# Pair-wise cross-attention mixture kernel: softmax weights turned by VectorE, first x loaded by rows, later x loaded earlier, GpSimd's setup reordered

## The chip, the core and the metric

The kernel runs on one NeuronCore of one Trainium2 chip. The metric is the device time of one execution, in microseconds, and the number to predict is the median of timed executions. Engine names below are those of the profile: PE is TensorE (PEld its weight loads), DVE is VectorE, ACT is ScalarE, POOL is GpSimd, and SP is SyncE, which here only issues DMAs.

## What is computed

x has shape (8, 512, 256): 8 batches of 512 tokens, with 64 context vectors for each batch and one conditioning vector, the anchor. All of it is 32-bit. In short:

```
nx       = layer_norm(x, gamma, beta)
weights  = softmax((nx @ Wq) (context @ Wk)^T / 16)          # 512 x 64 for each batch
evidence = weights @ (context @ Wv)
combined = [nx, evidence, anchor]                             # 768 wide
probs    = softmax(combined @ router_W + router_b)            # 3 experts
h_e      = silu(combined @ e_w1[e] + e_b1[e])                 # 768 -> 512, for each expert
routed   = sum_e probs_e * (h_e @ e_w2[e] + e_b2[e])          # 512 -> 256
g        = sigmoid(silu(combined @ gate_w1 + gate_b1) @ gate_w2 + gate_b2)
out      = x + g * (routed @ out_w + out_b)
```

## The kernel before

**Folding.** The key and query matrices are joined into one, so the scores are one product of nx with a 256 x 64 matrix for each batch. The value matrix is folded into the evidence rows of the first layers (`vw`), so the product with the evidence becomes a product of the softmax weights `wT` (64 context rows by 512 tokens) with `vw`. The second layers are folded with `out_w` (`w2o`). The router's softmax needs only logit differences against expert 0.

**Pairs.** The eight batches are handled as four pairs `j`. A pair is a 2 x 2 block matrix (two halves of the features by two batches), and each product of it is done with seven block products in place of eight. The extra sums and differences of weights are made once by POOL (`combine_weights`, `ws`), those of x by DVE or POOL (`combine_x`, tile `T`).

**Stages of a pair.** `gate_layer` makes the hidden layer of the gate. `expert_layer` runs three times, for the three experts, with the points "W", "A", "B", "C" and "D" at which other steps are hung. `outputs` does the second layers, with the points "begin", "gate", "P1" to "P7". The lists `within` and `between` at the end of the program say which step is run at which point: the next pair's statistics, normalization, scores, softmax and router logits lie between the products of the current pair. Every engine runs its instructions in the written order, and SP's DMAs are issued in the written order too.

**Names that matter below.**
- `load_x` (L139) loads one tile x by four DMAs of 32 partitions; partition quarter (i, h) holds half h of the tokens of batch i of the pair. With this layout the softmax weights, made with tokens on partitions in 32 x 32 blocks, have their router sums by token. The tag "x" has two buffers, so pair j+1's two tiles wait for the readers of pair j's.
- `statistics`, `deviation`, `normalize` (L528 to L550) are the layer norm; `store_x`, `regroup_x` and `transpose_blocks` bring x of later pairs into the transposed form `nxT` through DRAM; `transpose_x` (L562) does it by TensorE for the first pair.
- `router_part` (L586) makes the last logit difference of a tile from x and a row `gg`, by four DVE instructions. For the first pair it is hung at "gate".
- `scores` (L628), `softmax` (L659) and `turn_weights` (L666): the weights w are normalized with tokens on partitions; `turn_weights` transposes them in 32 x 32 blocks into `tw`, and DMAs carry the blocks to the partitions of `wT`. For the first pair four DMAs are issued by ACT, after two DVE transposes; for later pairs eight are issued by SP.
- `router_logits` (L682) needs the router's rows `vr`, which go from `vw` through DRAM (`store_router_rows`, `spread_router_rows`, both on POOL's queue), and `rbias`, which goes the same way (`router_anchor`, `spread_router_bias`).
- `misc` (L104) hands out PSUM banks in turn from a short list, so a new user of a bank waits for the readers of the one before.

Of the kernel before, what the change touches and what calls it, by code (L numbers as in the profile page):

```python
# [8 lines left out]
F32 = mybir.dt.float32  # L9
# [7 lines left out]
def kernel(  # L17
# [121 lines left out]
    def load_x(b):  # L139
        x_sb[b] = xpool.tile([P, NT, H], F32, tag="x", name=f"x_{b}")  # L140
        j, a = b // 2, b % 2
        for i, h in SIDES:
            nc.sync.dma_start(x_sb[b][side(i, h), :, :], tile_rows(x[2 * j + i], a, h))
# [15 lines left out]
    def by_k(flat, n):  # L159
# [16 lines left out]
        scr[:, NL : NL + 3 * KH * E].rearrange("p (k e) -> p k e", e=E),  # L176
        scr[:, NL + P : NL + P + KH * ED].rearrange("p (k e) -> p k e", e=ED),
        scr[:, NL + 2 * P : NL + 2 * P + B],
# [94 lines left out]
    nc.gpsimd.memset(rw2, 0.0)  # L273
    nc.gpsimd.tensor_copy(rw2[:, :, 1:], rwd[:, :KH, 1:])
    nc.gpsimd.tensor_tensor(rb_c[:, 0:1], rb_c[:, 0:1], rb_c[:, 1:], ALU.subtract)
# [98 lines left out]
    def router_anchor():  # L374
        ps = misc("ps_rb")
        for k in range(KH):
            nc.tensor.matmul(
                ps[:ED, :B], rwd[:, 2 * KH + k, :], condT[:, k, :B], start=(k == 0), stop=(k == KH - 1)
            )
        for k in range(KH):  # L380

            nc.tensor.matmul(
                ps[:ED, B : B + 1], rw2[:, k, :], beta_c[:, k : k + 1], start=(k == 0), stop=(k == KH - 1)
            )
        nc.vector.tensor_scalar(rcol, ps[:ED, B : B + 1], rb_c[:, 0:1], None, ALU.add)
        nc.vector.tensor_scalar(
            rrow.rearrange("e (i j) -> e j i", i=2), ps[:ED, :B].rearrange("e (j i) -> e j i", i=2),
            rcol, None, ALU.add,
        )
        nc.gpsimd.dma_start(rbd.rearrange("i j e -> e (i j)"), rrow)  # L390
# [171 lines left out]
    def transpose_x(b):  # L562
        j, a = b // 2, b % 2
        xn = S["xn", b]
        for k in range(KH):
            if a == 0:
                row = 2 * j + k
                S["nxT", row] = npool.tile([P, KH, T], F32, tag="nxT", name=f"nxT_{row}")
        for k in range(KH):
            pt = misc(f"pt_x_{b}_{k}")  # L570
            for t in range(NT):
                nc.tensor.transpose(pt[:, t * P : (t + 1) * P], xn[:, t, k * P : (k + 1) * P], ident)
            src = pt.rearrange("p (j i h r) -> p i h j r", i=2, h=2, r=TB)
            for i in range(2):
                dst = S["nxT", 2 * j + i][:, k, :]
                dst = dst.rearrange("p (h a j r) -> p a h j r", h=2, a=2, r=TB)[:, a]
                scale_x(dst, k, src[:, i], k % 2 == 0)

# [7 lines left out]
    def router_part(b):  # L586

        j, a = b // 2, b % 2
        lg = logits(j)
        junk = work.tile([P, H], F32, tag="tw", name=f"junk_{b}", bufs=1)  # L590
        for t in range(NT):
            nc.vector.scalar_tensor_tensor(  # L592
                junk, S["xn", b][:, t, :], 1.0, gg, ALU.mult, ALU.mult,
                accum_out=lg[:, 2, a * NT + t : a * NT + t + 1],
            )
# [32 lines left out]
    def scores(j):  # L628


        ps = misc(f"ps_s_{j}")
        for g in range(2):
            for k in range(KH):
                for i, h in SIDES:
                    nc.tensor.matmul(
                        ps[side(i, h), g * NH : (g + 1) * NH],
                        mr[:, k, 2 * j + i, g * TB : (g + 1) * TB],
                        S["nxT", 2 * j + i][:, k, h * NH : (h + 1) * NH],
                        start=(k == 0),
                        stop=(k == KH - 1),  # L640
                    )
        w = work.tile([P, 2, NJ, TB], F32, tag="w", name=f"w_{j}", bufs=1)
        S["w", j] = w
        nc.vector.transpose(w.rearrange("p g j c -> p (g j c)"), ps)
        nc.vector.tensor_copy(logits(j)[:, 1, :], w[:, 0, :, 0])
        nc.vector.memset(w[:, 0, :, 0], 0.0)
        mx = work.tile([P, NJ], F32, tag="mx", name=f"mx_{j}")
        nc.vector.tensor_reduce(mx, w.rearrange("p g j c -> p j g c"), AX.XY, ALU.max)
        nmx = work.tile([P, NJ], F32, tag="nmx", name=f"nmx_{j}")
        nc.vector.tensor_scalar_mul(nmx, mx, -SCALE)  # L650
        sm = work.tile([P, NJ], F32, tag="sm", name=f"sm_{j}")
        for t in range(NJ):
            nc.scalar.activation(
                w[:, :, t, :], w[:, :, t, :], AF.Exp, bias=nmx[:, t : t + 1], scale=SCALE,
                accum_out=sm[:, t : t + 1],
            )
        S["sm", j] = sm

    def softmax(j):  # L659
        w, sm = S["w", j], S.pop(("sm", j))  # L660
        rs = work.tile([P, NJ], F32, tag="rs", name=f"rs_{j}")
        nc.vector.reciprocal(rs, sm)
        rs = rs.unsqueeze(1).unsqueeze(3).to_broadcast([P, 2, NJ, TB])
        nc.vector.tensor_tensor(w, w, rs, ALU.mult)

    def turn_weights(j, queue, twice=False):  # L666

        tw = work.tile([P, 2, NH], F32, tag="tw", name=f"tw_{j}", bufs=1)
        nc.vector.transpose(
            tw.rearrange("p g t -> p (g t)"), S["w", j].rearrange("p g j c -> p (g j c)")  # L670
        )
        wT = work.tile([P, T], F32, tag="wT", name=f"wT_{j}", bufs=1)
        S["wT", j] = wT
        if twice:

            nc.vector.transpose(wT, S["w", j].rearrange("p g j c -> p (g j c)"))
        for i, h in SIDES:
            for g in range(2):
                if not twice or g != h:
                    queue.dma_start(wT[side(i, g), h * NH : (h + 1) * NH], tw[side(i, h), g, :])  # L680

    def router_logits(j):  # L682
        w, lg, vr = S["w", j], S["lg", j], S["vr", j]
        le = work.tile([P, ED, NJ], F32, tag="le", name=f"le_{j}")
        for e in range(ED):
            pv = work.tile([P, 2, NJ, TB], F32, tag="tw", name=f"pv_{j}_{e}", bufs=1)
            nc.vector.tensor_tensor(
# [173 lines left out]
    def gate_layer(j, steps):  # L861
# [12 lines left out]
        keep_part(n, 1, 1, Z[n])  # L874
        if j == 0:
            turn_weights(0, nc.scalar, twice=True)
        nx_product(j, n, 2, True)
# [300 lines left out]
    with tc.manual_schedule(engines=None):  # L1178
# [36 lines left out]
        store_router_rows(0)  # L1215
        spread_router_bias()
        combine_weights(E)
        spread_router_rows(0)
        transpose_x(1)
        combine_x(0, nc.vector, (0, 1))  # L1220
        scores(0)
        load_table(AF.Silu)
        combine_weights(0)
        softmax(0)
        value_weights(0, 0, nc.vector.tensor_copy)
        anchor_rows(E)
        anchor_rows(0)
        combine_x(0, nc.vector, (2, 3))
        combine_weights(1)
# [9 lines left out]
        for j in range(NP):  # L1239
# [7 lines left out]
            if j == 0:  # L1247
                put(within, "gate", router_part, 0)
                put(within, "gate", router_part, 1)
                put(within, "gate", value_weights, 0, 1)  # L1250
# [20 lines left out]
            if j:  # L1271
                put(within, "gate end", spread_probabilities, j)
            put(within, (0, "C" if j == 0 else "B"), value_weights, j, 2)
            put(within, (1, "C"), load_x_blocks, 2 * j)
            put(within, (2, "A"), gate_differences, j)
            put(within, (2, "C"), load_x_blocks, 2 * j + 1)
            if j + 1 < NP:
                b0, b1 = 2 * j + 2, 2 * j + 3
                put(within, "gate", load_x, b0)
                put(within, "gate", load_x, b1)  # L1280
                put(within, (0, "A" if j else "D"), statistics, b0, 0, NT)
                put(within, (0, "B") if j else (1, "A"), statistics, b1, 0, NT)
                for i in range(2):
                    put(within, (0, "D") if j else (1, "C"), deviation, j + 1, i)
                for b, n in ((b0, (1, "W") if j else (1, "D")), (b1, (1, "A") if j else (2, "W"))):
                    put(within, n, normalize, b)
                    put(within, n, store_x, b)
                put(within, (1, "C") if j else (2, "A"), regroup_x, b0)
                put(within, (1, "B") if j else (2, "A"), router_part, b0)
                put(within, (2, "W") if j else (2, "B"), router_part, b1)  # L1290
                put(between, "begin", transpose_blocks, b0)
# [9 lines left out]
                put(between, "P7", router_logits, j + 1)  # L1301
                put(between, "P7", turn_weights, j + 1, nc.sync)
                put(between, "P3", value_weights, j + 1, 1)
                put(between, "P3", router_exp, j + 1)
                put(between, "P4", router, j + 1)
# [38 lines left out]
```

## Time and profile before

| | |
|---|---|
| timed runs | 496.11, 498.0 and 501.9 us, median 498.0 |
| the profiled execution | 503.33 us, of which 501.5 us is the span from its first to its last instruction |
| granted TensorE clock, mean | 0.975 |
| PE, DVE, ACT, POOL busy | 94%, 72%, 43%, 19% of the span |
| setup and first gate layer | 0 to 54.5 us |
| pair 0 from expert 0 to its outputs' end | 54.5 to 171 us |
| pairs 1, 2, 3 | from 171, 285 and 394 us |

The profiled execution is slower than the slowest timed run by 1.4 us, so differences worked out from its rows are taken from 503.33, and the same difference is then taken from the median. In a row of the timeline the first number is the start and the second the duration of the group (both in us), then come engine, line, operation, tiles, and in brackets the idle time of the engine before it with what ended it. A 128x512 product is two PE records in this trace, which at full rate start 0.43 us apart.

### The profile page before, as it was taken

What the parts mean: (1) busy time and instruction counts of PE and PEld (TensorE: products, weight loads), DVE (VectorE), ACT (ScalarE), POOL (GpSimd) and SP (SyncE); (2) the same over time, 40 slices, a digit from 0 to 9 for tenths busy, and PEclk for the clock granted to TensorE, in tenths of its full rate; (3) what the DMA queues carried; (4) which work ended last, traced back from release to release, by engine and by line L of the source; (5) the groups of instructions that cost most, each with busy time, mean ns of one, the idle gap of its engine ahead of it and who ended that gap; (6) DMA issues with size and microseconds to landing.
All of it is one profiled execution on the core that took longest, in us unless ns stands there. A gap on an engine that the chain in (4) does not pass through costs nothing.

```text
span 501.5 us, 4762 instructions
## 1 busy us (share of the span) xinstructions
PE 473.0 (94%) x1439; PEld 213.6 (43%) x1439; DVE 361.6 (72%) x668; ACT 215.2 (43%) x385; POOL 96.9 (19%) x132
## 2 busy tenths in 40 slices
PE   8874999997999996999999998999999999999996
PEld 6531354632444442443444443443444444444454
DVE  2854474797879935789888954988979925787972
ACT  2440465543822253655822154745622364468000
POOL 5239012410107220000107230000108210000020
PEclk9988799998999998999999999999999999999999
DMA  9995723034201272181201182470201391000013
GB/s 216 286 171 112 136 35 127 1 90 78 43 5 21 40 193 64 48 141 22 43 5 22 36 195 64 100 111 0 42 7 21 60 211 25 0 0 1 0 21 64
DMA packets 120795, 35.81 MB, mean 71 GB/s; under 512 B 106605, under 2 KB 117793, under 8 KB 120257
## 3 DMA queue, kind: packets, MB, share of 16 engines
q1 hardware_dynamic: 116560, 27.81, 29.3%
q0 software_dynamic: 2128, 6.78, 4.3%
q10 hardware_dynamic: 2080, 0.92, 0.7%
q8 instruction: 11, 0.18, 0.2%
q14 instruction: 16, 0.12, 0.1%
HBM read 27.17 MB, written 7.39 MB: 69 GB/s over the span
## 4 chain that ended last, share of the span: by engine, by line
PE 59%; DVE 20%; DMA 12%; SPq 5%; issue 2%; ACT 1%; DVEq 0%
PE ps_u L774 30%; PE ps_z L774 11%; PE ps_y L774 9%; DMA x<-in_x_dram 5%; DMA ow_sb<-in_L_xcond_out_w_dram 4%; DVE h L1051 4%; PE ps_gu L774 3%; DVE h L858 3%; DVE junk L592 2%; PE ps_vw L749 2%; SPq L680 2%; SPq L1073 2%; PE ps_w2o L489 1%; PE ps_gz L774 1%; DMA w<-in_L_xcond_e_w_dram 1%
## 5 line engine op out<-in xcount | busy, mean ns | idle before, releaser
L858 DVE TENSOR_TENSOR h<-h,pb 128x512 f32<-128x512 f32 x96 | 62.0, 696 | 9.2 <-ACT h L807 9.2
L774 PE MATMUL ps_u<-h,w2o 128*128 128x512 f32 x144 | 64.1, 594 | 0.0
L807 ACT ACTIVATE h<-h,abias 128x512 f32<-128x512 f32 x72 | 49.3, 719 | 31.2 <-DVE h L813 31.1
L774 PE MATMUL ps_u<-nxT,w 128*128 128x512 f32 x112 | 57.4, 619 | 2.2 <-ACT hg L816 1.4
L774 PE MATMUL ps_z<-wT,vw 64*128 64x512 f32 x104 | 53.1, 642 | 0.0
L1084 POOL TENSOR_TENSOR yb<-yb,xb 128x512 f32<-128x512 f32 x14 | 18.4, 1317 | 140.4 <-DVE yb L1083 121.6
L774 PE MATMUL ps_z<-h,w2s 128*128 128x512 f32 x96 | 42.6, 593 | 0.2 <-DVE r L1067 0.2
L816 ACT COPY h<-ps_u 128x512 f32<-128x512 f32 x48 | 28.0, 583 | 33.9 <-PE ps_u L774 33.5
L774 PEld LDWEIGHTS ps_u<-h,w2o 128*128 128x128 f32 x144 | 27.1, 190 | 32.6 <-issue 29.2
L774 PE MATMUL ps_u<-T,w 128*128 128x512 f32 x56 | 29.9, 655 | 9.5 <-DVE h L813 9.5
L813 DVE TENSOR_TENSOR h<-h,ps_y 128x512 f32<-128x512 f32 x24 | 16.4, 682 | 26.7 <-PE ps_y L774 21.1
L403 POOL DMA_DIRECT2D vrd<-vw x8 | 5.0, 629 | 157.5 <-ACT vw L756 157.5
L1051 DVE TENSOR_TENSOR h<-h,h 128x1024 f32<-128x1024 f32 x24 | 34.3, 1486 | 0.0
L774 PEld LDWEIGHTS ps_u<-nxT,w 128*128 128x128 f32 x112 | 19.7, 191 | 34.1 <-issue 22.7
L774 PE MATMUL ps_u<-wT,vw 64*128 64x512 f32 x56 | 30.4, 659 | 4.1 <-DVE hg L813 4.1
L774 PE MATMUL ps_z<-T,ws 128*128 128x512 f32 x56 | 28.7, 594 | 3.4 <-POOL ws L230 3.4
L774 PE MATMUL ps_y<-wT,vw 64*128 64x512 f32 x56 | 29.6, 645 | 1.7 <-DMA wT<-tw 1.7
L774 PE MATMUL ps_y<-nxT,w 128*128 128x512 f32 x56 | 29.3, 606 | 0.0
L807 ACT ACTIVATE h<-ps_u,abias 128x512 f32<-128x512 f32 x24 | 16.4, 688 | 28.5 <-PE ps_z L774 28.5
L813 DVE TENSOR_TENSOR h<-h,ps_z 128x512 f32<-128x512 f32 x24 | 16.1, 686 | 17.1 <-PE ps_z L774 17.1
L774 PEld LDWEIGHTS ps_z<-h,w2s 128*128 128x128 f32 x96 | 18.1, 190 | 23.5 <-issue 21.8
L774 PE MATMUL ps_u<-T,ws 128*128 128x512 f32 x56 | 27.6, 611 | 0.0
(224 smaller groups left out, 805.8 us busy)
## 6 DMA issues: line engine op xcount, KB each, us to landing
pb<-pd POOLq DMA_DIRECT2D x4, 1536.0 KB, 8.1
x<-in_x_dram SPq DMA_DIRECT2D x32, 128.0 KB, 4.2
xb<-in_x_dram SPq DMA_DIRECT2D x64, 64.0 KB, 2.5
out_dram<-yb SPq DMA_DIRECT2D x56, 64.0 KB, 2.0
w<-in_L_xcond_e_w_dram SPq DMA_DIRECT2D x6, 512.0 KB, 11.8
xd<-x SPq DMA_DIRECT2D x24, 128.0 KB, 2.2
xg<-xd SPq DMA_DIRECT2D x48, 64.0 KB, 2.3
scr_wa<-in_L_xcond_e_w_dram SPq DMA_DIRECT2D x3, 512.0 KB, 20.2
```

The source lines that it names most:

```text
L489: nc.tensor.matmul(ps[:, d * H : (d + 1) * H], w2T[:, k, (i + d) * P : (i + d + 1) * P], ow_sb[:, k, :], start=(k == 0), stop=(k == KH - 1),)
L592: nc.vector.scalar_tensor_tensor(junk, S["xn", b][:, t, :], 1.0, gg, ALU.mult, ALU.mult, accum_out=lg[:, 2, a * NT + t : a * NT + t + 1],)
L680: queue.dma_start(wT[side(i, g), h * NH : (h + 1) * NH], tw[side(i, h), g, :])
L749: nc.tensor.matmul(ps, vT[:, k, j * 2 * CT : (j + 1) * 2 * CT], w1[:, KH + k, n0:n1], start=(k == 0), stop=(k == KH - 1),)
L774: nc.tensor.matmul(ps, lhsT, rhs, start=start, stop=True, skip_group_check=not start)
L807: nc.scalar.activation(h, h if src is None else src, AF.Silu, bias=abias[:, c, 2 * j + i : 2 * j + i + 1])
L813: nc.vector.tensor_tensor(h, h, part, ALU.add)
L816: nc.scalar.copy(chunk(n, i, d), part)
L858: nc.vector.tensor_tensor(h, h, S["pb", j][:, i, :, 2 * q // RC, :], ALU.mult)
L1051: nc.vector.tensor_tensor(d, p, m, ALU.subtract)
L1073: queues[m % len(queues)].dma_start(rows_out[:, :, lo : lo + TB], yb[m * TB : (m + 1) * TB, ts].rearrange("r (j c) -> r j c", c=TB),)
L1084: nc.gpsimd.tensor_tensor(yb, yb, S["xb", 2 * j + row][:, i, :], ALU.add)
```

## The change

1. `turn_weights` has no DMA any more. DVE transposes all of w into `wT`, then does four more transposes of 32 partitions by 256 elements that read one partition quarter and write another. It runs after `softmax(0)` for the first pair, in the setup, and at "P3" in place of "P7" for the later ones.
2. For the first pair x is loaded by rows: two DMAs of 128 partitions in place of eight of 32, and `transpose_x` makes one `nxT` from one x, with one scaling instruction of 512 columns for each half in place of two of 256.
3. The last router logit of the first pair comes from eight small products of TensorE (`pl` in `scores`) in place of eight `router_part` instructions of DVE at "gate". The bias of it changes accordingly in `router_anchor`.
4. The first pair's exponential is one ACT instruction over 512 columns, after a subtraction by DVE and followed by a sum by DVE, in place of eight with a running sum.
5. On POOL, `combine_weights(E)` and `combine_weights(0)` stand ahead of `spread_router_bias` and `spread_router_rows`. `combine_x` is split further.
6. x of pairs 2 and 3 is loaded at "begin" of the outputs of two pairs earlier, not at "gate" of the pair before.
7. `router_part`, `normalize` and `statistics` of the later pairs are hung at other points: for pair 1's x the second `router_part` goes from (2, "B") to (2, "C"); for later ones the second `normalize` goes from (1, "A") to (1, "W"), the first `router_part` from (1, "B") to (1, "A"), the second from (2, "W") to (1, "D").

```diff
     def load_x(b):
         x_sb[b] = xpool.tile([P, NT, H], F32, tag="x", name=f"x_{b}")
         j, a = b // 2, b % 2
+        if j == 0:
+            nc.sync.dma_start(x_sb[b], x[b].rearrange("(t p) d -> p t d", p=P))
+            return
...
+        if j == 0:
+            pl = misc("ps_l")[:, :NH]
+            for k in range(KH):
+                for i, h in SIDES:
+                    nc.tensor.matmul(
+                        pl[side(i, h), :], rw2[:, k, :], S["nxT", i][:, k, h * NH : (h + 1) * NH],
+                        start=(k == 0), stop=(k == KH - 1),
+                    )
...
+        if j == 0:
+            nc.vector.tensor_tensor(w, w, by_token(mx), ALU.subtract)
+            nc.scalar.activation(w, w, AF.Exp, scale=SCALE)
+            late = work.tile([P, NJ, TB], F32, tag="pv", name="logits_0", bufs=1)
+            nc.vector.transpose(late.rearrange("p j c -> p (j c)"), pl)
+            nc.vector.tensor_copy(logits(j)[:, 2, :], late[:, :, 0])
+            nc.vector.tensor_reduce(sm, tokens, AX.XY, ALU.add)
+            return
...
-    def turn_weights(j, queue, twice=False):
-        tw = work.tile([P, 2, NH], F32, tag="tw", name=f"tw_{j}", bufs=1)
-        nc.vector.transpose(
-            tw.rearrange("p g t -> p (g t)"), S["w", j].rearrange("p g j c -> p (g j c)")
-        )
-        wT = work.tile([P, T], F32, tag="wT", name=f"wT_{j}", bufs=1)
+    def turn_weights(j):
+        wT, w = work.tile([P, T], F32, tag="wT", name=f"wT_{j}", bufs=1), S["w", j]
         S["wT", j] = wT
-        if twice:
-            nc.vector.transpose(wT, S["w", j].rearrange("p g j c -> p (g j c)"))
+        nc.vector.transpose(wT, w.rearrange("p g j c -> p (g j c)"))
         for i, h in SIDES:
-            for g in range(2):
-                if not twice or g != h:
-                    queue.dma_start(wT[side(i, g), h * NH : (h + 1) * NH], tw[side(i, h), g, :])
+            nc.vector.transpose(
+                wT[side(i, 1 - h), h * NH : (h + 1) * NH],
+                w[side(i, h), 1 - h, :, :].rearrange("p j c -> p (j c)"),
+            )
...
         store_router_rows(0)
-        spread_router_bias()
         combine_weights(E)
-        spread_router_rows(0)
         transpose_x(1)
         combine_x(0, nc.vector, (0, 1))
         scores(0)
         load_table(AF.Silu)
         combine_weights(0)
+        spread_router_bias()
+        spread_router_rows(0)
         softmax(0)
         value_weights(0, 0, nc.vector.tensor_copy)
+        turn_weights(0)
+        combine_x(0, nc.vector, (2,))
         anchor_rows(E)
         anchor_rows(0)
-        combine_x(0, nc.vector, (2, 3))
+        combine_x(0, nc.vector, (3,))
...
-                put(within, "gate", router_part, 0)
-                put(within, "gate", router_part, 1)
...
+            if j and j + 1 < NP:
+                put(within, (0, "B"), statistics, 2 * j + 3, 0, NT)
...
-                put(within, "gate", load_x, b0)
-                put(within, "gate", load_x, b1)
+                if j == 0:
+                    put(within, "gate", load_x, b0)
+                    put(within, "gate", load_x, b1)
+                if j + 2 < NP:
+                    put(between, "begin", load_x, b0 + 2)
+                    put(between, "begin", load_x, b1 + 2)
...
-                put(within, (1, "B") if j else (2, "A"), router_part, b0)
-                put(within, (2, "W") if j else (2, "B"), router_part, b1)
+                put(within, (1, "A") if j else (2, "A"), router_part, b0)
+                put(within, (1, "D") if j else (2, "C"), router_part, b1)
...
-                put(between, "P7", turn_weights, j + 1, nc.sync)
                 put(between, "P3", value_weights, j + 1, 1)
+                put(between, "P3", turn_weights, j + 1)
```

## The prediction

> **What bounds it now.** I read the page first. PE is busy 94% of the span, so time is won only where PE stands still or runs slowly.
>
> ```profile
> span 501.5 us, 4762 instructions
> ...
> PE 473.0 (94%) x1439; PEld 213.6 (43%) x1439; DVE 361.6 (72%) x668; ACT 215.2 (43%) x385; POOL 96.9 (19%) x132
> ...
> PEclk9988799998999998999999999999999999999999
> ```
>
> The granted clock dips in the first 60 us. Next I read PE's timeline over the whole span for rows with an idle time in brackets. Those over 1 us are all of these:
>
> ```profile
> 31.32 1.12 PE L774 MATMUL ps_z<-T,ws 128*128 128x512 f32 x2 [3.41 <-POOL ws L230]
> 39.79 1.12 PE L774 MATMUL ps_u<-nxT,w 128*128 128x512 f32 x2 [1.35 <-ACT hg L816]
> 42.64 1.15 PE L774 MATMUL ps_y<-wT,vw 64*128 64x512 f32 x1 [1.72 <-DMA wT<-tw]
> 50.80 1.22 PE L774 MATMUL ps_u<-wT,vw 64*128 64x512 f32 x1 [4.08 <-DVE hg L813]
> ...
> 116.91 2.96 PE L774 MATMUL ps_u<-T,w 128*128 128x512 f32 x4 [3.28 <-DVE h L813]
> ...
> 197.71 3.78 PE L774 MATMUL ps_u<-T,w 128*128 128x512 f32 x4 [3.89 <-DVE h L813]
> ...
> 309.66 1.98 PE L774 MATMUL ps_u<-T,w 128*128 128x512 f32 x4 [2.36 <-DVE h L813]
> ```
>
> Four holes of 10.6 us together lie in the first gate layer, three of 9.5 us in later stages. The duration behind each hole matters too: four records take 1.98 us at 309.66 and 3.78 us at 197.71, half the rate. What holds PE up is in the other engines' rows of the same timeline:
>
> ```profile
> 29.16 1.05 POOL L394 DMA_DIRECT2D rbias<-rbd  x2 [6.59 <-DMA rbd<-scr_k]
> 30.80 0.47 POOL L230 TENSOR_TENSOR ws<-w 128x128 f32<-128x128 f32 x1
> ...
> 34.86 4.25 ACTq L680 DMA_DIRECT2D wT<-tw  x4
> 37.55 1.06 POOL L411 DMA_DIRECT2D vr<-vrd  x2 [4.07 <-DMA vrd<-vw]
> 43.62 0.74 DVE L592 SCALAR_TENSOR_TENSOR junk<-x,gg 128x256 f32<-128x256 f32 x1 [8.79 <-DMA wT<-tw]
> ...
> 190.32 0.43 DVE L535 BATCH_NORM_STATS2 st<-x 128x6 f32<-128x256 f32 x1 [5.16 <-DMA x<-in_x_dram]
> ```
>
> So: POOL's weight sums (L230) stood behind two small DMAs that they don't need; ACT's queue was held 4.25 us by issuing the turn's DMAs, with PE's next copy behind them; DVE stood idle 8.79 us until those DMAs had read the buffer that `junk` shares with `tw`, and then did eight `router_part` instructions (43.6 to 49.4) ahead of the adds that PE waited for; and pair 1's third tile of x came 5.16 us too late.
>
> **Part by part: the first gate layer.** In the trace expert 0 begins on PE at 54.5. I rebuild that point with the durations of before.
> - x by rows: DVE's first statistics waited for x until 10.24. The eight issues of SP took 5.27 us; two at about 0.5 each take 1, and the weights behind them in SP's queue go out up to 4 us sooner. But the transpose of x is held by PE's own queue until 13.3 (small transposes, whose rows come through POOL's queue), so I take only 1 us: scores end at 23.1, not 24.07. Bounds: 0 (x limited by the DMA engines, busy 9 tenths there) to 2.
> - `pl`: eight 32-column products. The scores' sixteen took 1.93 us (32 records at 150.4), so eight cost 0.95 on PE, which then does `vw` 1.72 and the anchor rows 0.87: the gate's first product at 26.7, as before (26.8).
> - POOL: `combine_weights(E)` (0.47+0.45+0.90+0.85 = 2.7 us) runs from about 22, as its gate weights had landed at 13.8. `ws` is there at 25, and the 3.41 us hole goes. The moved bias DMAs land later by little: `rbd` landed only at 29.2 and `vrd` at 37.5 in any case, and the sums of expert 0 now fill POOL until then.
> - Softmax: eight activations took 2.8 us (26.2 to 29.0). Now a subtraction 0.70, one activation 0.72, a sum 0.69 (512-column rows L664, L807, L648). From scores at 23.1: transpose, copy, maximum to 25.0, those three to 27.2, reciprocal and product to 28.2, `vw` copy and difference to 29.4.
> - The turn: one transpose of 512 columns at 0.70, and four of 256 columns on 32 partitions, an operation that has no row. [...] I take the time from the columns: the 64-partition, 256-column row L763 takes 0.42 us where 128x512 takes 0.69, so half the partitions save nothing, and 256 columns cost 0.42. With partitions free the four cost nothing extra beside one of 256 columns, 0.4; as full-cost instructions, 1.7; a partition move that streams slowly could cost 1 us each, 4. I take 1.7, the nearest row: `wT` at 31.8, against 42.6 before. ACT issues nothing.
> - Then DVE: the split `combine_x` 0.84, two anchor transposes 0.45, to 33.1. PE did its five products by 31.0 and now waits: by the order of PSUM banks `value_weights(0, 1)` takes the bank that the second anchor transpose reads. So a new hole of 2.1 us, then 1.72 + 0.86, and evidence 3.44: expert 0 begins at 39.1.
>
> That is 15.4 us won. I take off 0.9 for a slow clock behind the new hole: **14.5 us**. What is late next: `router_logits` at expert 0's point "A", DVE at about 45, needs `vr`, which would land at 43 to 44 (landing of `vrd` 37.5, issue 1.06, 5.1 to landing). The cover is 1 us; if it is gone, DVE's adds queue behind it and PE waits with them. The second-layer weights (`load_second(0)`, last issue 43.4, landing 2.5 later) are read at 49. SP loads x of pair 1 a little sooner, with no `router_part` to wait for.
>
> **Pair 0, expert 2.** DVE is in arrears from 92.4 to 121.7. Four `router_part` instructions, 1.74 us, stand before the adds of 116.17; at (2, "C") they stand behind. The hole of 3.28 becomes 1.5. They are not removed, but DVE idles 2.1 and 1.0 us at 123 to 127, which takes them. [...] After 3.28 the rows show 0.98 us lost in the four records and 0.78 in the evidence behind, 1.76 in all. By the holes alone this part gives 1.7; by rule and rows **3.5 us**, which I take.
>
> **Pairs 1 and 2, expert 0.** x is loaded some 65 us sooner, while DMA engines are 1 to 2 tenths busy. SP issues eight DMAs (4.0 us, row at 180.78) behind `load_x_blocks` and ahead of `regroup_x`, where SP waits for a DVE transpose anyway (17.3 us the longest such wait); stores come later. So free. DVE's statistics, 2.4 us a tile, then run at 185.2 and 188.3, and the add that was at 197.0 stands at about 191.5, before PE asks at 193.8. The hole of 3.89 goes, with its half-rate stretch (1.8 in the four records, 0.9 in the evidence): **6.6 us**. At 309.66 only the hole goes: **2.4 us**. The moved `normalize` and `router_part` put `add(a)` of expert 1 2 us later (209.7 to 211.7); ACT's copy that PE needs at 213.7 is then done at 213.0, so nothing. Cover gone, up to 1 us a pair.
>
> **The turn of later pairs** stands at "P3", 1.7 us more on DVE, in a stage where PE has no hole (122 to 182) but DVE has little room:
>
> ```profile
> 176.75 0.69 DVE L813 TENSOR_TENSOR hg<-hg,ps_u 128x512 f32<-128x512 f32 x1 [0.37 <-PE ps_u L774]
> ```
>
> That add comes 1.3 late; PE's evidence into the same bank starts at 178.46, 1.0 after the add's end. Together they cover 1.4. `wT` would be ready at 174, needed at 176.6. Removing eight issues of SP (5.04 us) only brings stores forward. Between 0 and 1.3 for each transition I take 0.5: **1.5 us lost**.
>
> Sum: 14.5 + 3.5 + 6.6 + 2.4 - 1.5 = 25.5. The profiled execution, 503.3, becomes 477.8; the median, 498.0, becomes **473**.
>
> **Rivals.**
> - *Router rows late.* Setup DMAs are saturated (`vrd`'s 0.5 KB took 15.7 us). If `vr` lands 3 to 6 us later, DVE stalls in expert 0 and PE with it, plus a half-rate stretch of 2 to 3: 478 to 484. For: POOL's queue; against: earlier issue of all weights. Chance 0.18.
> - *VectorE becomes the bound between pairs.* If the quarter transposes cost 1 us each, a transition loses 2.6 and perhaps a half-rate stretch: three times 2 to 4 more, 479 to 487. For: 0.37 us of room; against: the column rows. Chance 0.15.
> - *Slower.* The same instructions at a much higher price: 16 quarter transposes stand in DVE's order ahead of what PE waits for. The rest of the change gives about 33 us (25.5 + 1.5 + 4 x 1.7), so from 2.4 us each (33 + 5 us, over 16) it is over 1% slower: 503 to 510. For: no row shows a DVE write to other partitions; against: every transposing row follows its columns. Chance 0.04.
> - *It does not do what it says*: another wait stands behind each hole removed, 493 to 503. Seven holes with four different releasers speak against that. Chance 0.03.
> - *More*: the x loads, no new hole, no lost transition, below 466. Chance 0.05.
>
> The forecast itself, 466 to 478, has 0.55.
>
> **Range.** A measurement tells about 1% (5 us) from no change: three timed runs of before spread over 1.2%. From 464 to 485, which leaves out the slow and no-change cases and the ends of two others. Faster 0.93, within 1% 0.03, slower 0.04.
>
> **What would show it.** Right: expert 0's first product near 39 to 41; no bracket over 1 us before it but one of about 2 at `value_weights`; quarter transposes near 0.4; no wait of `st` for `x`; first expert stages of pairs 1 and 2 without holes. Wrong: a DVE wait for `vr` or `rbias`, quarter transposes over 0.7, or a new PE hole at 171 to 182 (shifted) that ends with DVE `hg`.

## The result, and the profile after

The changed kernel takes 472.4 us (median of 6 runs, 472.06 to 474.32) against 499.95 us for the kernel before, run beside it (6 runs, 494.66 to 502.77). The ratio is 0.950, with a 95% interval of 0.944 to 0.956. The prediction was 473 us from a median of 498.0. Its profiled execution has a span of 470.6 us, against 501.5. Ratios here leave out executions over 1.5% above the fastest of their kernel, so they can differ a little from a quotient of the medians.

The page of the changed kernel, span, busy time and granted clock:

```profile
span 470.6 us, 4723 instructions
...
PE 461.1 (98%) x1455; PEld 209.8 (45%) x1455; DVE 362.1 (77%) x669; ACT 213.3 (45%) x368; POOL 95.0 (20%) x133
...
PEclk9999999999999999999999999999999999999999
```

PE has 16 more instructions and yet 11.9 us less busy time: the stretches at half rate are gone, and the clock no longer dips in the first 60 us. The rest of the 30.9 us, 19.0, is idle time. PE's timeline over the whole span, the rows with over 1 us idle before them (behind PE's first instruction):

```profile
32.13 1.98 PE L763 MATMUL ps_vw<-w,vT 128*128 128x512 f32 x4 [1.52 <-DVE ar L438]
...
98.34 1.98 PE L788 MATMUL ps_u<-T,w 128*128 128x512 f32 x4 [1.53 <-DVE h L827]
```

Seven holes have become two of 1.5 us, both followed by full rate (four records in 1.98 us), and both at places that the prediction named: at `value_weights`, where it expected 2.1, and in pair 0's expert 2, where it expected 1.5. What stood behind the old holes, in the other engines' rows of the same timeline:

```profile
8.57 0.43 DVE L540 BATCH_NORM_STATS2 st<-x 128x6 f32<-128x256 f32 x1 [2.33 <-DMA x<-in_x_dram]
...
21.19 0.52 POOL L233 TENSOR_TENSOR ws<-w 128x128 f32<-128x128 f32 x1
...
28.48 0.71 DVE L689 STREAM_TRANSPOSE wT<-w 128x512 f32<-128x512 f32 x1
29.23 1.78 DVE L691 STREAM_TRANSPOSE wT<-w 32x256 f32<-32x256 f32 x4
...
35.11 1.06 POOL L416 DMA_DIRECT2D vr<-vrd  x2 [3.18 <-DMA vrd<-vw]
...
43.98 0.65 DVE L701 TENSOR_TENSOR pv<-w,vr 128x512 f32<-128x512 f32 x1
```

Row by row: x's first statistics start 1.7 us sooner (10.24 before); `ws` starts at 21.2, not 30.8; `wT` is whole at 31.0, not 42.6, and the four quarter transposes cost 0.44 us each, where 0.42 was taken; the router row `vr` is issued 2.4 us sooner than before, and its reader at 43.98 has no wait in brackets, so the 1 us of cover held.

By stretches of PE's program, from its first product of each stretch (start of span, expert 0, outputs) in the two traces:

| stretch | before | after | gained | predicted |
|---|---|---|---|---|
| start to pair 0's expert 0 | 54.51 | 38.54 | 15.97 | 14.5 |
| pair 0's experts | 67.87 | 63.63 | 4.24 | 3.5 |
| pair 1's experts | 55.76 | 48.41 | 7.35 | 6.6 |
| pair 2's experts | 51.61 | 48.41 | 3.20 | 2.4 |
| three stretches from outputs to the next expert 0 | 173.65 | 174.50 | -0.85 | -1.5 |
| the rest (pair 3's experts, its outputs) | 98.14 | 97.16 | 0.98 | 0 |
| span | 501.5 | 470.6 | 30.9 | 25.5 |

The first stretch gained more than its holes. From the gate's first product to expert 0, the two kernels have these sums (stretch, its length, PE's busy time and instructions, granted clock, DMA share and GB/s), before and after:

```profile
26.78:54.51 27.73, 17.16 (x36) 0.79 0.75 147
...
26.05:38.54 12.49, 10.97 (x37) 1.00 0.83 142
```

PE's busy time fell by 6.2 us for one more instruction: that is, in the main, the slow clock behind the holes. Its idle time fell by 9.1 us, from 10.6 to 1.5.

The medians differ by 27.6 only. The profiled execution of before, 503.33, was one of its longer ones; the experiments below bear on what makes them differ.

### The profile page after: what moved, and what is told of

It reads as the page before. It is cut to its first block, busy times and chain, and to the rows that moved or that the text cites. A ratio compares the mean times of both kernels' runs of the same rounds, so it can differ in the third digit from the quotient of the medians.

```text
span 470.6 us, 4723 instructions
## 1 busy us (share of the span) xinstructions
PE 461.1 (98%) x1455; PEld 209.8 (45%) x1455; DVE 362.1 (77%) x669; ACT 213.3 (45%) x368; POOL 95.0 (20%) x133
## 2 busy tenths in 40 slices
DMA packets 119351, 34.86 MB, mean 74 GB/s; under 512 B 106060, under 2 KB 116352, under 8 KB 118816
## 4 chain that ended last, share of the span: by engine, by line
PE 67%; DVE 26%; issue 3%; DMA 3%; POOL 0%; ACT 0%; DVEq 0%; POOLq 0%; ACTq 0%
PE ps_u L788 32%; PE ps_z L788 12%; PE ps_y L788 12%; DVE h L1063 5%; PE ps_gu L788 3%; DVE h L872 3%; PE ps_vw L763 3%; DVE r L1094 2%; DVE yb L1095 2%; DVE r L1093 2%; DVE wT L691 1%; PE ps_w2o L494 1%; PE ps_gz L788 1%; DMA scr_small<-in_L_xcond_router_W_dram 1%; DMA scr_small<-in_L_xcond_e_b_dram 1%
## 5 line engine op out<-in xcount | busy, mean ns | idle before, releaser
L788 PE MATMUL ps_u<-nxT,w 128*128 128x512 f32 x112 | 55.9, 608 | 0.5 <-ACT h L830 0.5
L788 PE MATMUL ps_z<-wT,vw 64*128 64x512 f32 x104 | 49.5, 605 | 0.0
L788 PE MATMUL ps_z<-h,w2s 128*128 128x512 f32 x96 | 42.6, 593 | 0.2 <-DVE r L1079 0.2
L788 PE MATMUL ps_u<-wT,vw 64*128 64x512 f32 x56 | 28.2, 617 | 0.5 <-DVE hg L827 0.4
L763 PE MATMUL ps_vw<-w,vT 128*128 128x512 f32 (+1 forms) x64 | 27.0, 544 | 1.5 <-DVE ar L438 1.5
L788 PE MATMUL ps_u<-T,w 128*128 128x512 f32 x56 | 26.7, 594 | 1.5 <-DVE h L827 1.5
L788 PE MATMUL ps_y<-wT,vw 64*128 64x512 f32 x56 | 27.0, 597 | 0.0
```

Source lines behind the costliest of these rows:

```text
L763: nc.tensor.matmul(ps, vT[:, k, j * 2 * CT : (j + 1) * 2 * CT], w1[:, KH + k, n0:n1], start=(k == 0), stop=(k == KH - 1),)
L788: nc.tensor.matmul(ps, lhsT, rhs, start=start, stop=True, skip_group_check=not start)
```

## The experiments

They ask of each term of the sum whether the step that it names is the cause. The base is the changed kernel, or, where said, the kernel before. The expectations name earlier experiments by number, e1 to e12, which stands in each heading.

### The first gate layer

**The first turn by DMA again, on ACT's queue at the gate layer (e2).**

```diff
-        turn_weights(0)
...
+        if j == 0:
+            turn_by_dma(0, nc.scalar)   # transposes into tw and wT, four DMAs tw -> wT
```

> The changed kernel with the first pair's turn put back: two DVE transposes at the gate layer and four DMAs issued by ACT. My theory: ACT is held 4.3 us and wT lands some 6 us after the issue, evidence starts at about 40 in place of 34.9, perhaps with a slow clock behind: 477 to 482 us. Rival, the first gate layer is bound by the setup's other DMAs and the turn was hidden: under 2 us, 472 to 474.

Measured: 483.01 us (482.29 to 484.35), 10.6 above the changed kernel, just over what was expected. Expert 0 begins at 49.55, 11.0 later. Timeline rows of this kernel:

```profile
30.96 0.70 DVE L698 STREAM_TRANSPOSE tw<-w 128x512 f32<-128x512 f32 x1
...
37.94 4.63 ACTq L705 DMA_DIRECT2D wT<-tw  x4
42.62 0.58 ACT L841 COPY hg<-ps_u 128x512 f32<-128x512 f32 x1 [13.80 <-DMA scr_w<-in_L_xcond_e_w_dram]
43.25 2.08 PE L799 MATMUL ps_u<-nxT,w 128*128 128x512 f32 x2 [11.11 <-ACT hg L841]
```

`tw` is complete at 31.7 and `wT`'s own part at 32.3, but ACT's four issues start at 37.94, take 4.63 us, and only then comes the copy that PE waits for. One hole of 11.1 us replaces what had been four, and half rate follows (two records in 2.08 us, where 1.12 is usual). The profile puts the wait ahead of the issues down to a weight DMA of SP's. Why an issue on ACT should wait for it no run shows. The kernel before did not have this wait: there ACT's issues began at 34.86, when DVE had just written `wT`'s own part:

```profile
34.16 0.67 DVE L676 STREAM_TRANSPOSE wT<-w 128x512 f32<-128x512 f32 x1
```

So some 5.7 us of the 10.6 (37.94 less 32.25) belong to this experiment alone, and the turn by DMA itself costs about 5 us here, an estimate by subtraction.

**POOL's order of before (e3)**, with `spread_router_bias` and `spread_router_rows` around `combine_weights(E)`:

```diff
         store_router_rows(0)
+        spread_router_bias()
         combine_weights(E)
+        spread_router_rows(0)
...
         combine_weights(0)
-        spread_router_bias()
-        spread_router_rows(0)
```

> The changed kernel with POOL's setup order put back (small router DMAs ahead of the gate's weight sums). My theory: the second gate product waits for the sums until about 30 to 31, a hole of some 3 us, partly the same time as the hole of 1.5 at the value weights: 474 to 478 us. Rival, POOL was off the path: 472 to 473.

Measured: 474.54 us (473.83 to 475.74), 2.1 more. The hole is back in PE's timeline, almost at its old size,

```profile
30.27 1.12 PE L788 MATMUL ps_z<-T,ws 128*128 128x512 f32 x2 [3.18 <-POOL ws L233]
```

but the hole of 1.52 at `value_weights` is gone in turn, so expert 0 is 1.6 late, not 3.2.

**The same order alone, in the kernel before (e6):** the two `spread` steps moved behind `combine_weights(0)` and nothing else.

> The kernel before with one thing done: POOL's weight sums ahead of the small router DMAs. My theory now: the holes of the first gate layer are not all additive; what ends it is the turn's DMAs and then router_part on DVE, and neither waits for POOL's sums, so the 3.4 us hole moves behind the others: 0 to 1.5 us less than the kernel before. Rival, as my sum had it, each hole is time won: 3 to 5 us less.

Measured: 500.83 us (494.65 to 504.51) beside 500.23 (496.51 to 507.03), ratio 0.996 (0.991 to 1.001): no gain. PE's timeline:

```profile
42.04 2.08 PE L774 MATMUL ps_u<-nxT,w 128*128 128x512 f32 x2 [7.35 <-ACT hg L816]
...
50.04 1.22 PE L774 MATMUL ps_u<-wT,vw 64*128 64x512 f32 x1 [3.14 <-DVE hg L813]
```

The hole of 3.41 for `ws` is gone, and the one for ACT's copy has grown from 1.35 to 7.35: PE comes sooner to the same wait. Expert 0 begins 0.75 sooner.

**Eight DVE instructions of 128x256 with a sum put back at "gate" (e8)**, of the kind that `router_part` has (their results are not used):

```diff
             if j == 0:
+                put(within, "gate", extra_work, 0)
+                put(within, "gate", extra_work, 1)
                 put(within, "gate", value_weights, 0, 1)
```

> The changed kernel with eight extra DVE instructions of the router_part kind (128x256, with a sum, results unused) at the first gate layer, where router_part stood; everything else stays. My theory: 8 x 0.5 to 0.6 us, of which DVE's idle 1.9 us ahead of the adds takes a part: 2 to 4 us longer, 474 to 477. Rival, the adds are not what PE waits for there: 472 to 473.

Measured: 475.05 us (473.72 to 475.44), 2.6 more; expert 0 1.9 late. PE waits where it waited 4.08 us before:

```profile
38.51 0.69 PE L797 MATMUL ps_u<-wT,vw 64*128 64x512 f32 x1 [2.05 <-DVE hg L836]
```

The three undone parts cost 10.6 (about 5 without the added wait), 2.1 and 2.6 us, and one of them done alone brings nothing. The four holes of the prediction's view were stations of chains that run side by side (POOL's sums, the turn with ACT's queue, DVE's work), and the longest sets expert 0. Loading x by rows and the split exponential were not tried alone.

### Pair 0, expert 2

**The second `router_part` back at (2, "B") (e11)** in the changed kernel:

```diff
-                put(within, (1, "D") if j else (2, "C"), router_part, b1)
+                put(within, (1, "D") if j else (2, "B"), router_part, b1)
```

> The changed kernel with pair 1's second router_part back at (2, B) of pair 0. My theory, from the prediction: the hole in expert 2 of pair 0 grows from 1.5 to 3.3 us and half rate follows, 3.5 us in all: 475 to 476.5. By the holes alone 474.2. Rival, DVE's arrears only move: 472 to 473.

Measured: 476.57 us (475.48 to 477.88), 4.2 more. PE's timeline:

```profile
100.29 3.78 PE L788 MATMUL ps_u<-T,w 128*128 128x512 f32 x4 [3.28 <-DVE h L827]
```

The hole grew by 1.75 us and the four records behind it by 1.80; the evidence products that follow took 1.0 more. So more than half of this part's price is rate and not the hole.

### Pairs 1 and 2, expert 0

The prediction's reason was that x, issued long before it is needed (pair 2's at 102.9 in the changed kernel, at 160.3 with this undone), lands in time. **Undo that alone (e1):**

```diff
-                if j == 0:
-                    put(within, "gate", load_x, b0)
-                    put(within, "gate", load_x, b1)
-                if j + 2 < NP:
-                    put(between, "begin", load_x, b0 + 2)
-                    put(between, "begin", load_x, b1 + 2)
+                put(within, "gate", load_x, b0)
+                put(within, "gate", load_x, b1)
```

> The changed kernel with one thing undone: x of pairs 2 and 3 is loaded again at the gate layer of the pair before. My theory: late x made the holes of pairs 1 and 2, so their first expert stages lose again what they won (7.4 and 3.2 us between the two traces): 481 to 484 us. Rival, the moved DVE steps won it: at most 3 us, 473 to 476.

Measured: 472.54 us (472.2 to 472.84), as the changed kernel. The expected 481 to 484 was missed altogether: x loaded late costs nothing here. Something else must have made it late before. One candidate was SP's queue, from which the turn's eight DMAs are gone. **With x late, eight DMAs that nobody needs were put on SP's queue at "P7" (e9):**

```diff
                 put(between, "P7", router_logits, j + 1)
+                put(between, "P7", extra_dmas, j + 1)   # eight DMAs of 32 KB, w -> DRAM
```

> The changed kernel with x of pairs 2 and 3 loaded late again (as in e1) and with eight extra DMAs of the size of the turn's (32 partitions x 1 KB, to DRAM, unused) on SP's queue at P7, where the turn's stood. New theory: what made x late in the kernel before was not the place of load_x alone; the turn's eight DMAs held SP about 5 us, so that the last x DMAs were issued after the 1.5 MB broadcast of the router's probabilities and landed behind it. Then the holes in expert 0 of pairs 1 and 2 return: 477 to 483 us. Rival, e1 lost nothing because the later turn on VectorE moved the broadcast or because the statistics stand elsewhere: 472 to 473.5.

Measured: 473.05 us (472.77 to 474.74). The additional DMAs were issued from 146.5 to 150.2, and x at 159.8 to 163.2, no later than without them. The 477 to 483 expected did not come: SP's queue does not make x late.

From the other side, **early x alone, in the kernel before (e5)** (the same lines as above, the other way round):

> The kernel before with one thing done: x of pairs 2 and 3 loaded at the outputs two pairs earlier. My theory: 9 to 10 us less than the kernel before (6.6 + 2.4 by its rows). Rival, the moved DVE steps are needed too: under 3 us less.

Measured: 496.32 us (493.53 to 498.07) beside 500.23, ratio 0.992 (0.988 to 0.996). That is 3.9 us, not the 9 to 10 expected, though in its trace the two holes are 0.51 each. And **the later pairs' turn by DVE alone, in the kernel before (e10)**, which also takes the eight DMAs from SP:

```diff
-                put(between, "P7", turn_weights, j + 1, nc.sync)
                 put(between, "P3", value_weights, j + 1, 1)
+                put(between, "P3", turn_by_vector, j + 1)
```

> The kernel before with one thing done: the turn of pairs 1 to 3 by VectorE at P3, without DMAs. New theory: SP is free sooner and the broadcast goes out later, so x lands ahead of it though it is loaded late, and the holes in expert 0 of pairs 1 and 2 go as with early loading: 4 to 8 us less than the kernel before. Rival, only early loading does that: 0 to 1.5 us more than before, for the lost room of VectorE.

Measured: 499.52 us (496.42 to 501.07) beside 500.85 (496.2 to 506.04), ratio 1.001 (0.997 to 1.005): no difference. Its trace did show the holes smaller, 1.59 and 0.53. What differs in it is the issue of the router probabilities' broadcast to all partitions, 1.5 MB on POOL's queue (`pb`):

```profile
L143 SPq DMA_DIRECT2D x<-in_x_dram x8: 430/430/1776, 179.6 to 184.3; - x8
...
L743 POOL DMA_DIRECT2D pb<-pd x1: 565/565/565, 183.7 to 183.7; - x1
```

It went out ahead of only the last two of x's eight DMAs for pair 2. For pair 3, where the hole is 0.53, it went out behind all eight.

That led back to the trace of before. What it says of x's eight DMAs for pair 2, issued in pair 1, and of the broadcast (issue times, then time to landing):

```profile
L143 SPq DMA_DIRECT2D x<-in_x_dram x8: 430/432/642, 180.8 to 184.2; - x8
...
DMA to landing us min/median/max: 2.6/8.2/9.0
...
L733 POOL DMA_DIRECT2D pb<-pd x1: 567/567/567, 182.5 to 182.5; - x1
```

The three issued first landed after about 2.7 us; all from 182.29 on, issued about when the broadcast went out or later, after 7.8 to 9.0. The fourth of them completes pair 2's first tile, and this is the wait of 5.16 us on `st` that the prediction showed (and took for one of pair 1's tiles). **So the broadcast was moved behind x, in the kernel before, and x left late (e12):**

```diff
-                put(within, "gate end", spread_probabilities, j)
+                put(within, (0, "A"), spread_probabilities, j)
```

> The kernel before with one thing moved: the spreading of the router's probabilities (a 1.5 MB broadcast at its end) of pairs 1 to 3 from the gate layer's end to expert 0's point A, so that it goes out some 6 us after x, which stays late. Theory left after e1, e5, e9 and e10: x was late because its last DMAs were issued behind that broadcast. Then the holes in expert 0 of pairs 1 and 2 fall below 0.6 us, and the time is that of early loading in the kernel before (e5): 495 to 498 us. Rival, x is late by its own issue: the holes stay and the time is that of the kernel before, 499 to 502.

Measured: 493.92 us (12 runs, 493.09 to 495.4) beside 498.62 (17 runs, 492.84 to 505.88); ratio 0.995 (0.992 to 0.998); that is below the 495 to 498 expected. The same view for this kernel:

```profile
L143 SPq DMA_DIRECT2D x<-in_x_dram x8: 430/430/502, 180.3 to 183.7; - x8
...
DMA to landing us min/median/max: 2.7/3.0/3.6
...
L733 POOL DMA_DIRECT2D pb<-pd x1: 567/567/567, 188.3 to 188.3; - x1
```

and PE's timeline at the two places:

```profile
193.66 1.98 PE L774 MATMUL ps_u<-T,w 128*128 128x512 f32 x4 [0.53 <-DVE h L813]
...
301.31 1.98 PE L774 MATMUL ps_u<-T,w 128*128 128x512 f32 x4 [0.53 <-DVE h L813]
```

The holes went from 3.89 and 2.36 to 0.53 with x issued at the old time. It was late because the broadcast went out in the midst of its DMAs. In the changed kernel with x late (e1), the broadcast goes out behind all of x:

```profile
L146 SPq DMA_DIRECT2D x<-in_x_dram x8: 430/431/501, 160.3 to 163.7; - x8
...
L747 POOL DMA_DIRECT2D pb<-pd x1: 555/555/555, 164.3 to 164.3; - x1
```

Counted from pair 1's expert 0 it goes out at 3.4 us, where it was 1.8 before, and x is issued 0.7 us sooner. With the turn by DVE alone (e10) it is 3.5 us, so it is the turn's new form and place that hold the broadcast back. Early loading and this shift each cure the same delay, so undoing one shows nothing. That the shift is what protects the changed kernel is read from these issue times; no run takes both away.

### The turn of later pairs

**The four quarter transposes done twice for pairs 1 to 3 (e7):**

```diff
-        for i, h in SIDES:
-            nc.vector.transpose(...)
+        for _ in range(2 if j else 1):
+            for i, h in SIDES:
+                nc.vector.transpose(...)
```

> The changed kernel with the four quarter transposes done twice for pairs 1 to 3: 1.7 us more of DVE in each of three transitions. My theory: the room that DVE had there (1.4 us by the rows of before) is used up, so 1 to 1.7 us longer each time: 475 to 478 us. Rival, DVE has more room than I took: 472 to 473.5.

Measured: 481.35 us (479.76 to 481.76), above the 475 to 478 expected: 9 us for 5.2 us more of DVE's work (three times 1.74). First the changed kernel as it is, at pair 1's transition:

```profile
152.46 1.80 DVE L691 STREAM_TRANSPOSE wT<-w 32x256 f32<-32x256 f32 x4
...
157.82 0.67 DVE L827 TENSOR_TENSOR hg<-hg,ps_u 128x512 f32<-128x512 f32 x1
...
158.54 0.69 PE L788 MATMUL ps_u<-wT,vw 64*128 64x512 f32 x1
```

DVE's add follows the instruction before it with no idle time. PE's record ahead of the one shown starts at 157.82 too, and records follow one another at 0.43 here, so PE waits 0.3 us for DVE: no room is left. With the double turn, PE at the same place, and at the transitions to pairs 2 and 3:

```profile
160.76 0.84 PE L789 MATMUL ps_u<-wT,vw 64*128 64x512 f32 x1 [2.02 <-DVE hg L828]
...
162.25 1.05 PE L789 MATMUL ps_y<-wT,vw 64*128 64x512 f32 x1
...
270.85 0.69 PE L789 MATMUL ps_u<-wT,vw 64*128 64x512 f32 x1 [2.13 <-DVE hg L828]
...
379.26 0.89 PE L789 MATMUL ps_u<-wT,vw 64*128 64x512 f32 x1 [2.10 <-DVE hg L828]
```

All of DVE's addition becomes a hole, and behind two of the three the products run at half rate (records of 1.05 us, where 0.59 is usual) for over 3 us. The transitions lose 3.3, 1.9 and 3.4 us.

Three holes of nearly the same length, and only two are followed by half rate. How they lie to the instants at which the granted clock changes tells them apart. In the trace of before it changes eleven times, from 32.45 to 500.07, and the changes follow one another at 3.41 us or a whole multiple of it (6.83, 61.44, 75.09, 296.96). In the trace of the double turn the stretches at half the clock behind the first and the third hole begin 218.46 us apart, 64 times 3.413. This trace, cut from those instants into windows of that length, has around the three holes (length, PE's busy time, granted clock):

```profile
core 0: us, PE busy (x), PEclk, DMA share, GB/s
157.76:161.17 3.41, 1.39 (x8) 1.00 0.05 8
161.17:164.59 3.42, 3.42 (x9) 0.50 0.48 75
...
266.99:270.40 3.41, 1.73 (x8) 1.00 0.00 0
270.40:273.82 3.42, 2.97 (x11) 1.00 0.51 80
376.21:379.63 3.42, 1.32 (x8) 1.00 0.04 9
379.63:383.04 3.41, 3.41 (x9) 0.50 0.73 114
```

The first and the third hole lie inside one window each, PE is idle for 2.0 and 2.1 us of it, and the next window has half the clock. The second hole is split between two windows, 1.68 and 0.45 us, and the clock stays.

### A faster version

**Taking away the two holes that are left (e4):** the anchor rows ahead of the first turn, and for pair 0 the other `router_part` at (2, "C") too.

```diff
-        turn_weights(0)
-        combine_x(0, nc.vector, (2,))
         anchor_rows(E)
         anchor_rows(0)
+        turn_weights(0)
+        combine_x(0, nc.vector, (2,))
...
-                put(within, (1, "A") if j else (2, "A"), router_part, b0)
+                put(within, (1, "A") if j else (2, "C"), router_part, b0)
```

> The changed kernel with two steps moved: the anchor rows' transposes ahead of the first turn (so that the value weights' PSUM bank is free sooner), and pair 1's first router_part from (2, A) to (2, C) in pair 0. My theory: the two holes of 1.5 us that are left go: 469 to 471 us. Rival, another wait takes their place (the split difference of x behind the turn, DVE's arrears): 472 to 473.

Measured: 469.89 us (6 runs, 469.72 to 470.41), ratio to the kernel before 0.941 (0.936 to 0.946). It is faster than both kernels, than the changed one by 2.5 us. Expert 0 begins at 36.98. Of the 3.05 us of holes, some comes back: DVE still owes the moved work, and its longest new wait on PE is

```profile
117.20 1.98 PE L788 MATMUL ps_u<-h,w2s 128*128 128x512 f32 x4 [0.82 <-DVE h L1063]
```

## Why the prediction was right, and where its steps were not

**First gate layer: right in its path, 1.5 us too small.** Expert 0 was rebuilt to begin at 39.1 and begins at 38.54. Most of the difference is the 0.9 us taken off for a slow clock behind the new hole, which didn't come: after 1.52 us PE ran at full rate. x by rows gave 1.7 us at the statistics and about as much at the scores, where 1 was taken. The rebuilt path, not the list of holes, is what made this hold: the holes add up to 10.6 us, while the stretch gained 16.0, of which 6.2 is matrix products no longer at half rate, and the POOL order alone gained nothing. Which of the edits brought how much of it is not shown: their prices overlap.

**Pair 0, expert 2: right.** 3.5 was taken, 4.24 measured in the traces, and 4.2 when it was undone. The choice to count the slow stretch and not only the hole (1.7) was the right one. What the prediction calls "by rule and rows" is carried by the rows alone, 1.74 us of `router_part` and 1.76 lost behind the hole; no run shows such a rule. What the runs showed in its place is that the length of a hole alone doesn't settle it: the product behind the hole of 1.72 already takes 1.15 us, where 0.69 is usual, and behind that of 2.36 four records take 1.98, full rate. The windows of before, cut from the changes of its clock (columns as in the double turn's view), show how much of the holes falls into one of them:

```profile
39.27:42.69 3.42, 1.18 (x3) 1.00 0.71 141
42.69:46.10 3.41, 3.41 (x7) 0.50 0.44 69
...
114.37:117.78 3.41, 0.87 (x2) 1.00 0.78 123
117.78:121.19 3.41, 3.41 (x7) 0.50 0.69 110
...
305.51:308.93 3.42, 1.78 (x5) 1.00 0.02 7
308.93:312.34 3.41, 2.68 (x8) 1.00 0.00 0
```

2.5 us of the 3.28 did, and 2.2 us of the 1.72 and the 1.35 ahead of it, and half the clock followed; of the 2.36 it was 1.6 us, and the clock stayed.

**Pairs 1 and 2: the size in the trace was near (9.0 against 10.6), the step was wrong, so the size was luck.** The prediction wrote that x is loaded sooner, that statistics then run early, and that the hole goes. Early x would do it, but the delay came from the broadcast that had been issued between x's DMAs, which the prediction never looked for, and the changed kernel is free of it even with x late. Nor is all of the 10.6 from x: in the traces of early x alone and of the broadcast moved, the same two stretches gain 7.8 us. The other 2.7 us, 0.8 in expert 0 and 0.56 in expert 2 of each pair, are in neither of these traces and not in that of the turn alone, and they stay in the changed kernel with x late. That leaves DVE's moved steps, which the prediction put at nothing; they were not tried alone. In time the term is also too large. The experiments that cure only this bring 3.9 us (early x) and 4.7 us (broadcast moved) between medians, and, by their ratios, 2.3 to 5.9 and 0.8 to 3.8 us. Whether x falls behind the broadcast hangs on some tenths of a microsecond. The times fit that: before spreads from 492.8 to 505.9, and with the broadcast moved 12 runs spread over 2.3 us near the fast end of that. A rival for part of the spread, not shown, is where the other holes fall in such windows: with early x, which has no such race, ten runs still spread over 4.5 us. That the race makes up the rest is argued, not shown, since only one execution of each has a trace. Why the turn alone gained nothing in time, with smaller holes in its trace, stays open for the same reason.

**The turn of later pairs: right.** 1.5 us was taken, 0.85 measured (0, 0.39 and 0.46). The prediction's bound of 1.4 us of cover stands: what is added beyond the change is lost in full.

**The total.** In the traces 25.5 was 5.4 too small. Of the 30.9 some 3.4 belong to a profiled execution of before that was longer than the median (503.33 against 499.95), and the other 2.0 to the median taken as the base, 498.0, which was 499.95 in the runs beside the changed kernel. So 473 came this close to 472.4 because errors of opposite sign met, on top of a sum whose terms each had the right sign; being within 1 us was luck. The 1.0 us of the last stretch was not foreseen. The rows put it behind the last matrix product: ACT's last copy waits 0.3 us longer in before, for a DMA of the output, and before then ends 4.1 us after the start of its last DMA issue, the changed kernel 3.4. Nothing in the change explains it.

**The rivals.** Router rows late: no, DVE did not wait for `vr`. VectorE as the bound between pairs: not at 0.44 us a transpose, but the doubled turn shows how close it is; its price of 2 to 4 us a transition was about right. Slower: it needed 2.4 us for each quarter transpose, five times what they cost (the rest of the change adds up to 33.8 us there, not 33, which moves this little). Not doing what it says: for the POOL order alone this would have been the truth.

## What to carry to other kernels

Rebuild the path to the next point that matters and don't add up holes: those of parallel chains hide one another, so that one cure alone can be worth nothing and its undoing 2 us. When a small DMA lands late, list what else was issued in the microseconds around it on any queue, ahead of asking for an earlier issue. Where two edits could each cure a wait, undoing one shows nothing; do each alone in the old kernel too.

## What the runs showed of the hardware

- In the trace of before, x's DMAs of 128 KB for pairs 2 and 3 that SP issued 0.6 us or more ahead of a 1.5 MB broadcast on POOL's queue (seven) landed after 2.6 to 2.9 us; those issued 0.2 to 1.7 us behind it (seven), after 8.6 to 10.2 us; the two in between did either, 0.23 us ahead 3.3 and 0.17 us ahead 7.8. For pair 2 in other traces: all eight ahead of it, 2.9 to 3.1 us (e1) and 2.7 to 3.6 (e12); two behind it, 2.6 to 7.7 (e10); the broadcast in their midst, 3.1 to 10.3 (e6).
- A DVE transpose that reads one partition quarter and writes another takes 0.436 us for 32x256, against 0.712 for 128x512 in place (medians in the changed kernel's trace). The prediction's row of 256 columns that stays on its partitions takes 0.42, so no price of the change of partitions can be seen.
- How long a hole is doesn't alone tell whether PE then runs at half rate. Half rate followed holes of 2.02 and 2.10 us (e7) and one of 1.85 (e5: 1.7 us after its end two records take 1.87 us, where 1.09 is usual); full rate followed holes of 2.05 (e8), 2.13 (e7), 2.36 (before) and 3.18 (e3). In the traces of before and of the changed kernel, PE's idle time within one window of 3.41 us tells. Before's windows are cut from the changes of its clock; the changed kernel's clock has a single change, at 469.91, and its windows are cut from that with the same length. Of windows at full rate with another whole one behind them, counted from the clock's first record (5.1 and 5.7 us), before has 137: the five with 2.24 to 2.79 us of idle time were followed by half rate, the other 132, with 1.64 or less, by full rate. The changed kernel has 135, all with 1.52 or less and all followed by full rate. Before has seven windows at half rate: the five without idle time were followed by full rate, the two with 1.29 and 1.42 us by half rate again. How the hole of 3.18 us in e3 falls into windows is not shown.
